# Bursts of four fills in place of three in a causal-attention loop on one Trainium2 core

## The chip, the cores and the metric

The kernel runs on one core of a Trainium2 chip. The metric is the device time of one execution in microseconds (us); the time of the kernel before is the median of 3 runs. Besides the times there is one profiled execution with a trace of every instruction. The engines are named as in the profile: PE is TensorE (matmuls) and PEld its weight loads, DVE is VectorE, ACT is ScalarE, POOL is GpSimd, and SP is the engine that issues most DMAs.

## The reference

A block of three layers on x of 8 x 1024 x 256: half a feed-forward layer, causal attention with 16 heads of 16 columns, and half a feed-forward layer again, each added to x after a layer norm. Cut to the attention and to the fact that matters about the experts:

```python
def _L0_attn_ref(x, Wq, bq, Wkv, bkv, Wo, bo):
    q = x @ Wq.T + bq                       # 16 heads of 16 columns
    k, v = jnp.split(x @ Wkv.T + bkv, 2, axis=-1)
    dots = jnp.einsum('bhid,bhjd->bhij', q * scale, k)
    attn = softmax(where(causal, MASK_VAL, dots))
    return jnp.einsum('bhij,bhjd->bhid', attn, v) ... @ Wo.T + bo

def _L0_ffn_ref(tokens, gate_w, w1, b1, w2, b2):
    ...
    keep = counts <= cap                    # an expert over its capacity is dropped whole
    valid = keep[a_e]
    ...
x = x + 0.5 * _L0_ffn_ref(_layernorm(x), ...)
x = x + _L0_attn_ref(_layernorm(x), ...)
x = x + 0.5 * _L0_ffn_ref(_layernorm(x), ...)
```

An expert that gets more tokens than its capacity contributes nothing. The kernel counts the tokens of each expert on the chip and runs the feed-forward layers only if some expert is kept; on these inputs no expert is, so the profile shows one pass of attention with the gates' arithmetic beside it.

## The kernel before

**Units.** `attention` walks 32 units: 8 batches of 4 groups of 4 heads. In each unit there are 18 fills of a kind called maxima here (M, built by `m_steps`) and 18 called exponentials (E, built by `e_steps`). The M stream runs ahead: while the E fills of unit u run, the M fills of unit u+1 do, with a lead of three fills.

**An M fill** multiplies q and k into a tile `sm` of 128 x 1024 numbers in PSUM (a few 64-row matmuls on the two halves of the array), adds the causal mask by small bf16 matmuls where a diagonal block lies in it (10 of the 18 fills; the other 8 are called plain), and then VectorE takes the row maxima (`tensor_reduce` into `mx`). **An E fill** writes minus the maxima into a tile `sc` by a matmul (`sc<-neg,take_m`), adds k by q, and ScalarE takes the exponential into `pT`.

**Three buffers.** Both kinds of tile come from one pool, `ps_pair`, of three buffers of two PSUM banks; two more banks (`ps_sum`, `ps_bank`) serve everything else, so all eight are in use. Buffers go round: a fill takes the one that the third fill before it used, and its first matmul waits until VectorE or ScalarE has read that tile.

**Bursts and gaps.** The main loop emits fills by `step`, and after every third one (`FILLS = 3`, `every`) it calls `gap`. A gap emits the other work of TensorE: up to two pieces of attention times values that are due (`pav`, from the queue `owed`; one piece if at most two are queued), and steps of projections, values and output products (`pq`, `pv`, `px`, `pta`, from the queue `work`) at a rate of 17/12 a gap (13/12 for the first batch). These matmuls use the array in four column strips (128*32 in the profile), the fills use it in two row halves (64*128). The order of a unit's fills is written out: `"EMEMEM" * 6`, that is bursts E M E and M E M by turns, 36 fills and 12 gaps. At some places `small` steps of `side` work (layer-norm statistics, gate arithmetic, most of it on VectorE) go in. If six `pT` tiles are alive, an E fill first emits the next piece of `pav` itself.

**Order.** A `Lane` wraps each engine and pins every instruction behind the one before it in the source, so each engine's order is the order in which Python emits it. The program is written as straight-line code; all of it carries the helper's line L625 in the profile.

**DMAs.** The row maxima go out and back as DMAs (`rows<-mside`, `neg<-rows`); `fetch` brings the next unit's q and k (`qk<-parts`). Their places are counted in fills (`due`, `start`).

Of the kernel before, what the change touches and what calls it, by code (L numbers as in the profile page):

```python
# [29 lines left out]
def macaron_kernel(  # L30
# [570 lines left out]
    def attention(run_no, src, dst, gate0, logits, tally):  # L601
        NU = B * NG
        VW = HD + 1
        FILLS = 3
        stack = ExitStack()
        with stack:
            ps_pair = stack.enter_context(tc.tile_pool(name=f"ps_pair{run_no}", bufs=3, space=PSUM))
# [96 lines left out]
            def biased_late(b):  # L704
                for jj in range(TB // 2):
                    biased(b, jj)
                    yield
# [35 lines left out]
            def enter(b):  # L743
                xnT = xnTs[b] = ap.tile([P, DC, S], F32, tag="xnT", name=f"xnT{b}", bufs=1)
                for jj in range(TB // 2):
                    drain(coming.pop((b, jj), ()))
                    while (b, 2 * jj + 1) not in xns:
                        take(side)
                        yield
                    pt = bank(f"pta{b}_{jj}")  # L750
                    for i in range(2):
                        xn = xns.pop((b, 2 * jj + i))
                        for c in range(DC):
                            o = (c * 2 + i) * P
                            if b:
                                product(pt[:, o : o + P], xn[:, c * P : (c + 1) * P], ident)
                            else:
                                transpose(pt[:, o : o + P], xn[:, c * P : (c + 1) * P])
                    on.scalar.copy(
                        xnT[:, :, 2 * jj * P : (2 * jj + 2) * P], pt.rearrange("p (c w) -> p c w", c=DC)  # L760
                    )
                    if b and jj + 2 < TB // 2:
                        soon(b, jj + 2)
                    yield True
# [91 lines left out]
            def gate_first(b):  # L856
                if gate0 is not None:
                    lg = gate0[0][:, b * TB : (b + 1) * TB, :]
                    both = (yield from choose(ap_route, f"f{b}", TB, lg))[2]
                    on.vector.tensor_tensor(gate0[1], gate0[1], both, ALU.add)  # L860


            def m_steps(u):
                q, k = qks[u % 3][:, 0], qks[u % 3][:, 1]
# [39 lines left out]
                plain = [(1, [(ib, 0, pr, 0)]) for pr in range(2) for ib in range(4, 8)]  # L904
# [8 lines left out]
                if u == 0:  # L913
                    todo = masked_ones[0] + plain + masked_ones[1]
                else:
                    rest = deque(masked_ones[0] + masked_ones[1])
                    plain = deque(plain)
                    todo = [(plain if n % 3 == 1 or not rest else rest).popleft() for n in range(18)]
                steps = [lambda a=a: fill(*a) for a in todo]
                done = max(n for n, a in enumerate(todo) if a[0] == 0)  # L920

# [40 lines left out]
            count = [0]  # L962
# [237 lines left out]
            def mixed(many, few):  # L1200
                n = 0
                for step in many:
                    yield step
                    n += bool(step)
                    if step and n % 2 == 0:
                        for other in few:
                            yield other
                            if other:
                                break
                yield from few  # L1210
# [5 lines left out]
            def take(works):  # L1216
                while works:
                    try:
                        return next(works[0])
                    except StopIteration:  # L1220
                        works.popleft()
                return False
# [42 lines left out]
            def gap(rate):  # L1265
                n = 0
                most = 2 if len(owed) > 2 else 1
                while owed and n < most and owed[0][0] <= count[0]:
                    owed.popleft()[1]()
                    n += 1  # L1270
                behind[0] += rate
                while behind[0] >= 1:
                    behind[0] -= 1
                    if take(work) and not spare[0]:
                        break
                behind[0] = min(behind[0], 4)

            def step(fill, every, rate, small):
                due()
                fill()  # L1280
                count[0] += 1
                small, urgent[0] = max(small, urgent[0]), 0
                for _ in range(small):
                    if take(side):
                        break
                if count[0] % every == 0:
                    gap(rate)

            def start(steps, lag=0):
                timed.append([count[0] + (3 * lag + 2) // 4, steps])  # L1290

            def due():
                for entry in list(timed):
                    while entry[0] <= count[0]:
                        lag = next(entry[1], None)
                        if lag is None:
                            timed.remove(entry)
                            break
                        entry[0] = count[0] + (3 * lag + 2) // 4

            stream = [0]
            urgent = [0]
            units = {}

            def maxima():
# [13 lines left out]

            for u in range(-1, NU):  # L1320
                b, g = divmod(u, NG)
                rate, every = (17 if b else 13) / 12, FILLS
                if u < 0:
                    pass
                elif g == 0:
                    spare[0] = False
                    if b + 1 < B:
                        work += [enter(b + 1), project(b + 1, 0)]
                        if b:
                            work.append(mixed(leave(b - 1), project(b + 1, 1)))  # L1330
                        else:
                            work.append(mixed(values_of(b + 1), project(b + 1, 1)))
                        if b:
                            work.append(values_of(b + 1))
                    if b:
                        start(divide(b - 1, 1, 0), 4)
                        after[u - 1, 1] = divide(b - 1, 1, 1)
                    side.append(gate_first(b))
                    if not b:
                        side.append(biased_late(b))  # L1340
                elif g == 1 and b + 1 == B:
                    work.append(leave(b - 1))
                elif g == 1 and b == 0:
                    side.append(biased_late(1))
                elif g == 2:
                    if b == 0:
                        start(read(2), 40)
                    if b + 1 == B:
                        start(divide(b, 0, 0), 12)
                        start(divide(b, 0, 1), 16)  # L1350
                        after[u, 0] = divide(b, 1, 0, 4, (8, 1, 6, 8))
                elif g == 3:
                    if b + 1 < B:
                        start(divide(b, 0, 0), 8)
                        start(divide(b, 0, 1), 20)
                    if b + 1 == B:
                        after[u - 1, 1] = divide(b, 1, 1, 4, (6, 1, 4, 5))
                        last_on.append(ap.tile([P, 4, P], F32, tag="wsb", name="last_on", bufs=4))
                        on.gpsimd.memset(last_on[0], 0.0)
                        rate = 8 / 3  # L1360
                if u >= 0 and u + 2 < NU:
                    start(fetch(u + 2, lag=6), 8)
                if u < 0:
                    for n in range(18):
                        step(maxima, 1, 8 / 5 if n < 5 else 16 / 13, 1)
                else:
                    if u == 0:
                        for n in range(3):
                            step(maxima, every, rate, n)
                    es = deque(e_steps(u))  # L1370
                    for k, which in enumerate("EMEMEM" * 6):
                        small = 3 if k % 6 in (1, 5) else 0
                        if which == "E":
                            step(es.popleft(), 2 if u + 1 == NU else every, rate, 0 if u + 1 < NU else 2)
                        elif stream[0] < 18 * NU:
                            step(maxima, every, rate, small)
                if g == NG - 1:
                    while work and u + 1 < NU:
                        drain(work.popleft())
# [75 lines left out]
```

## Time and profile before

| | |
|---|---|
| median of 3 runs | 1188.32 us (1184.97 to 1193.11) |
| the profiled execution | 1189.08 us, span 1187.3 us, granted PE clock 0.985 of full speed |
| busy, ACT / POOL | 734.4 us (62%) / 432.9 us (36%) |
| DVE, from 350 to 950 us | 506.3 of 600 us busy |
| PE, from 350 to 950 us | 596.5 of 600 us busy |
| PE, from 1130 us to the end | 32.2 of 57 us busy |

A busy PE is not a PE at its peak: matmuls overlap, and their ends are modelled. What a stretch costs is read from the start of one matmul to the start of the next. A row of the timeline gives the start, the time from the first start to the last end of the merged instructions, the engine, the operation, the tiles (out<-in), the shape and how many there are; what ended the idle time before it stands in brackets.

### The profile page before, as it was taken

How to read it: one execution, taken by the hardware profiler on the slowest of the kernel's cores; microseconds unless marked ns; L12 is line 12 of the kernel's file. 1: busy time of each engine (PE TensorE's matmuls, PEld its weight loads, DVE VectorE, ACT ScalarE, POOL GpSimd, SP SyncE). 2: the span in 40 equal slices, each digit the busy share in tenths (PEclk: the TensorE clock that was granted, in tenths of full speed). 3: DMA queues.
4: the chain of work that ended last, by engine and by line, in shares of the span. 5: the costliest groups of instructions: out<-in, count | busy, mean ns of one | idle time of the engine just before them, and what ended most of it. 6: DMA issues, size and time to landing. Idle time of an engine off the chain costs nothing.

```text
span 1187.3 us, 36308 instructions
## 1 busy us (share of the span) xinstructions
PE 1132.9 (95%) x15178; PEld 657.9 (55%) x15178; DVE 936.8 (79%) x1652; ACT 734.4 (62%) x955; POOL 432.9 (36%) x774
## 2 busy tenths in 40 slices
PE   7789999999999999999999999999999999999983
PEld 4355555655565555655556555555556555555541
DVE  4667778788798878888888887988788887798934
ACT  4146666666666566666666666766666666665660
POOL 6125323433344223542235333442235423232331
PEclk9889999999999999999999999999999999999997
DMA  6553455565545557355564655455473555543211
GB/s 192 199 195 124 150 177 186 171 213 162 178 143 165 189 154 219 116 179 168 180 190 135 218 163 173 144 166 197 154 226 107 183 168 176 161 133 110 74 33 39
DMA packets 108517, 190.25 MB, mean 160 GB/s; under 512 B 24752, under 2 KB 42296, under 8 KB 108344
## 3 DMA queue, kind: packets, MB, share of 16 engines
q1 hardware_dynamic: 106968, 187.24, 49.4%
q8 instruction: 122, 2.00, 0.7%
q10 hardware_dynamic: 1376, 0.59, 0.2%
q14 instruction: 51, 0.42, 0.1%
HBM read 94.50 MB, written 93.31 MB: 158 GB/s over the span
## 4 chain that ended last, share of the span: by engine, by line
PE 80%; DMA 7%; DVE 7%; POOL 2%; ACT 1%; issue 1%; SPq 1%; ACTq 0%; POOLq 0%; DVEq 0%
PE sc L625 24%; PE pav L625 23%; PE sm L625 15%; PE pq L625 8%; PE pv L625 4%; PE px L625 4%; DVE mx L625 4%; PE pta L625 2%; DMA parts<-high 2%; DMA neg<-rows 1%; DMA parts<-split 1%; DMA rows<-mside 1%; DMA qk<-parts 1%; SPq L625 1%; POOL x_a L625 1%
## 5 line engine op out<-in xcount | busy, mean ns | idle before, releaser
L625 DVE TENSOR_REDUCE mx<-sm 128x2 f32<-128x1024 f32 (+2 forms) x576 | 686.5, 1217 | 167.6 <-PE sm L625 166.6
L625 ACT ACTIVATE pT<-sc 128x1024 f32<-128x1024 f32 x576 | 572.5, 1022 | 301.1 <-PE sc L625 292.2
L625 PE MATMUL pav<-pT,vaug 128*32 128x256 f32 (+3 forms) x4608 | 327.9, 387 | 2.2 <-ACT att L625 1.4
L625 POOL TENSOR_SCALAR_AFFINE_SELECT pT<-pT 128x256 f32<-128x256 f32 (+1 forms) x448 | 190.6, 441 | 308.5 <-ACT pT L625 307.2
L625 PE MATMUL sc<-neg,take_m 64*128 64x512 f32 x1152 | 265.7, 456 | 15.2 <-DVE mx L625 5.8
L625 PE MATMUL sm<-qk 64*128 64x512 f32 (+3 forms) x1536 | 264.7, 381 | 7.3 <-DMA qk<-parts 7.2
L625 PE MATMUL sc<-qk 64*128 64x512 f32 (+3 forms) x1536 | 229.6, 334 | 0.0
L625 PEld LDWEIGHTS sm<-qk 64*128 64x128 f32 x1536 | 139.5, 187 | 107.8 <-issue 47.5
L625 POOL TENSOR_TENSOR low<-whole,high 128x512 f32<-128x512 f32 x60 | 77.0, 1283 | 285.0 <-ACT high L625 278.8
L625 PEld LDWEIGHTS pav<-pT,vaug 128*32 128x32 f32 x4608 | 113.9, 109 | 104.6 <-issue 52.7
L625 PEld LDWEIGHTS sc<-neg,take_m 64*128 64x128 f32 x1152 | 109.9, 185 | 110.0 <-issue 56.2
L625 PEld LDWEIGHTS sc<-qk 64*128 64x128 f32 x1536 | 146.9, 186 | 15.6
L625 PE MATMUL sm<-masked,before_k 64*128 64x128 bf16 (+1 forms) x1280 | 86.9, 213 | 0.0
L625 PE MATMUL px<-woT,on 128*32 128x264 f32 x1024 | 74.8, 387 | 0.9 <-ACT on L625 0.9
L625 PE MATMUL pv<-wvT,xnT 128*32 128x264 f32 x1024 | 75.4, 391 | 0.0
L625 PE MATMUL pq<-xnT,wkT 128*32 128x256 f32 x1024 | 75.0, 389 | 0.0
L625 PE MATMUL pq<-xnT,wqT 128*32 128x256 f32 x1024 | 74.4, 389 | 0.5 <-ACT xnT L625 0.5
L625 PEld LDWEIGHTS <-before_k 64*128 64x128 bf16 x1280 | 38.5, 96 | 45.6 <-issue 29.9
L625 POOL TENSOR_TENSOR x_a<-x_a,bo_all 128x512 f32<-128x512 f32 x32 | 41.5, 1303 | 23.6 <-DVE xn_a L625 23.6
L625 PEld LDWEIGHTS pq<-xnT,wqT 128*32 128x32 f32 x1024 | 33.2, 112 | 29.2 <-issue 11.3
L625 PEld LDWEIGHTS px<-woT,on 128*32 128x32 f32 x1024 | 34.4, 110 | 26.8 <-issue 10.8
L625 PEld LDWEIGHTS pv<-wvT,xnT 128*32 128x32 f32 x1024 | 32.2, 110 | 26.3 <-issue 7.3
(133 smaller groups left out, 732.1 us busy)
## 6 DMA issues: line engine op xcount, KB each, us to landing
qk<-parts SPq DMA_DIRECT2D x124, 512.0 KB
parts<-high SPq DMA_DIRECT2D x120, 256.0 KB
parts<-low SPq DMA_DIRECT2D x120, 256.0 KB
sums<-att SPq DMA_DIRECT2D x62, 256.0 KB
out_dram<-x_a SPq DMA_DIRECT2D x16, 512.0 KB
x_a<-in_L_attn_x_dram SPq DMA_DIRECT2D x15, 512.0 KB
on<-sums SPq DMA_DIRECT2D x30, 256.0 KB
rs<-inv SPq DMA_DIRECT2D x30, 256.0 KB
```

Of the source, the lines that this page charges most:

```text
L625: i = call(*args, **kwargs)
```

## The change

The unit's order becomes `"MEEM" * 9`: M, two E, M, and then a gap. `FILLS` becomes 4, so that a unit has 9 gaps, and the rate of other work becomes 17/9 a gap (13/9 in the first batch). The two `small` places of three side steps in six fills become one of four in four, at the end of a burst. The count of fills at which a gap falls now starts where unit 0 begins (`first`). Within a unit's 18 M fills, plain and masked ones now alternate, and not one plain one among three.

```diff
-        FILLS = 3
+        FILLS = 4
...
-                    todo = [(plain if n % 3 == 1 or not rest else rest).popleft() for n in range(18)]
+                    todo = [(plain if (n % 2 == 1 and plain) or not rest else rest).popleft() for n in range(18)]
...
-                if count[0] % every == 0:
+                if (count[0] - first[0]) % every == 0:
                     gap(rate)
...
             urgent = [0]
+            first = [0]
...
-                rate, every = (17 if b else 13) / 12, FILLS
+                rate, every = (17 if b else 13) / 9, FILLS
...
                     if u == 0:
                         for n in range(3):
-                            step(maxima, every, rate, n)
+                            step(maxima, 1 if n == 2 else 99, rate, n)
+                        first[0] = count[0]
                     es = deque(e_steps(u))
-                    for k, which in enumerate("EMEMEM" * 6):
-                        small = 3 if k % 6 in (1, 5) else 0
+                    for k, which in enumerate("MEEM" * 9):
+                        small = 4 if k % 4 == 3 else 0
```

## The prediction

> **What bounds the kernel now.** I read the page's busy shares and its chain of waits first.
>
> ```profile
> PE 1132.9 (95%) x15178; PEld 657.9 (55%) x15178; DVE 936.8 (79%) x1652; ACT 734.4 (62%) x955; POOL 432.9 (36%) x774
> PE 80%; DMA 7%; DVE 7%; POOL 2%; ACT 1%; issue 1%; SPq 1%; ACTq 0%; POOLq 0%; DVEq 0%
> ```
>
> TensorE is busy nearly all the time and carries 80% of the chain that ended last; between 350 and 950 us it is busy 596.5 of 600. Whatever makes TensorE wait inside this loop lengthens the kernel, and whatever it no longer does shortens it.
>
> Second, the timeline of one burst M E M: what a change of array form costs, and when the first tile is read.
>
> ```profile
> 509.31 0.51 PE L625 MATMUL sm<-qk 64*128 64x512 f32 x2
> 509.64 0.39 PE L625 MATMUL sc<-neg,take_m 64*128 64x512 f32 x2
> 509.85 2.36 DVE L625 TENSOR_REDUCE mx<-sm 128x2 f32<-128x1024 f32 x2 [0.94 <-PE sm L625]
> 509.87 0.40 PE L625 MATMUL sc<-qk 64*128 64x512 f32 x2
> 510.10 0.40 PE L625 MATMUL sm<-qk 64*128 64x256 f32 x4
> 510.34 0.29 PE L625 MATMUL sm<-masked,before_k 64*128 64x128 bf16 x4
> 510.56 0.64 PE L625 MATMUL pav<-pT,vaug 128*32 128x256 f32 x8
> ```
>
> From start to start a pair of 512 columns takes 0.23 us (509.87 to 510.10), but the first of the burst 0.33. The three fills are through at 1.25. VectorE reads the first tile from 0.54 after the burst began, and two reductions take 2.36: the first ends at about 1.74. The burst is over by then, so TensorE doesn't care.
>
> Third, the one place after the start-up where six fills M E M E M E ran without a gap:
>
> ```profile
> 1067.26 0.50 PE L625 MATMUL sm<-qk 64*128 64x512 f32 x2
> 1067.62 0.50 PE L625 MATMUL sc<-neg,take_m 64*128 64x512 f32 x2
> 1067.96 0.40 PE L625 MATMUL sc<-qk 64*128 64x256 f32 x4
> ...
> 1068.34 2.34 DVE L625 TENSOR_REDUCE mx<-sm 128x2 f32<-128x1024 f32 x2
> ...
> 1069.61 0.50 PE L625 MATMUL sc<-neg,take_m 64*128 64x512 f32 x2 [0.84 <-DVE mx L625]
> 1069.94 0.39 PE L625 MATMUL sc<-qk 64*128 64x512 f32 x2
> ```
>
> The fourth fill needs the first fill's buffer. The first reduction ended near 1069.51 (half of 2.34 after 1068.34), the fourth fill began at 1069.61, and TensorE stood still for 0.84 us.
>
> **The change part by part.** All burst figures below are start-to-start times collected over every burst of the trace before. It has 398 bursts, which take 565 us from their first fill to the next other matmul: 153 of form E M E with a masked M (mean 1.617 us, 247 us), 153 M E M with a masked M at the end (1.353, 207), 31 + 31 without a mask (1.438 and 1.129, 80), and 30 others (31). The median pieces of M E M, masked, are 0.339 (first M), 0.468 (E) and 0.462 (masked M up to the next work).
>
> The changed kernel's instruction order, built but not run, has 338 bursts in the pass that executes: 217 M E E M with a plain first M and a masked last one, 30 with both masked, 30 M E E that break off because six `pT` tiles are alive (a piece of `pav` comes out, then M alone), 40 M alone (those 30, and 10 in the first unit's lead-in), and 21 odd ones. The number of matmuls is the same. So 60 bursts go, not the 96 that three gaps in each of 32 units would make.
>
> *What it removes.* Leaving a burst costs 0.09 (0.32 from the last `sc` to other work, 0.23 to another fill), entering costs 0.11 in the gap (0.31 in place of 0.20 between products) and 0.10 in the first fill: 0.30 a burst. Sixty times that is 18 us. A masked M in the middle costs the next E some 0.08 (E M E exits: 0.641 with a mask, 0.559 without); 153 such become 30: 123 x 0.08 = 10 us. The rest of what the sum below gains is that I put medians for the new bursts, without some 20 us that the means before hold over their medians (waits for `neg<-rows` and buffers; slower bursts give those DMAs more time).
>
> The Trainium skill, "TensorEngine Tiling (Array Packing)", Key Properties, says that a change of tiling mode drains the array, and "TensorE: Matmul & The Clock Gate", Single matmul latency, puts a drain near 175 ns. By that estimate two changes a burst would give 60 x 0.35 = 21 us where the rows give 18.
>
> *What it adds.* The wait. The changed order's semaphores say that each fill waits for the reader of the third fill before it: of a burst's last M that is the reduction of its own first M. Unstalled, that last M would start at 0.339 + 0.468 + 0.468 = 1.275. In the 184 bursts that begin with M now, the reduction starts 0.538 (tenth percentile), 0.543 (median), 0.63 (mean) after the burst and takes 1.22; it ends at 1.765, 1.770 and 1.85. A held fill restarts 0.05 to 0.10 after the reduction's end. So the last M starts at about 1.92 and TensorE waits 0.65, in each burst. It cannot be below 1.765 + 0.05, however idle VectorE is. Behind the held M stand, on TensorE's queue, the whole gap: `pav`, projections, output products, and ScalarE's evictions of those. Nothing can pass.
>
> A burst M E E M then takes 1.85 + 0.07 + 0.49 (0.46, and half of the 0.10 that a restart may pay) = 2.41. With a masked first M I add up 0.49 + 0.57 + 0.47 unstalled; its reduction ends near 1.91, and the burst takes 2.48. M E E: 0.339 + 0.468 + 0.55 = 1.36. M alone 0.82.
>
> Sum: 217 x 2.41 = 523, 30 x 2.48 = 74, 30 x 1.36 = 41, 40 x 0.82 = 33, others 19: 690 us against 565, +125. Sixty entries of 0.11 lie outside the bursts: -7. Together +118.
>
> The Trainium skill, "Perfetto Trace Analysis", Optimization Strategy, speaks against this change: the same bubble repeating on the saturated engine can mean that PSUM has no room for the next tile. It has no price for it.
>
> *What I cost at nothing.* The bunched side steps: VectorE's work a burst is 936.8/288 = 3.25 us; a burst and its gap will last some 4.4, so VectorE should be free when the next first M is done. If it isn't, each 0.1 us of lateness costs 247 x 0.1 = 25 us. ScalarE has two exponentials in a row (2 x 1.02, ending about 3.1 after the burst began); their buffers are wanted in the next burst, after 4.4. The gap's work is the same amount in nine pieces. SP's DMAs are placed by fills, and fills come slower.
>
> Bounds: with the reduction never late (1.765, restart 0.05, last M 0.46) M E E M takes 2.28; 30 x 2.40; the sum is 660, +88 in all. With VectorE 0.15 later than its mean now: 118 + 247 x 0.15 = +155.
>
> The profiled execution took 1189.08, 0.1% over the median; the forecast is 1189 + 118 = 1307.
>
> **The rivals.** *Faster: the last M doesn't wait.* If two E fills covered the reduction, the bursts would take 217 x 1.735 + 30 x 1.99 + 41 + 33 + 19 = 529 us, -36 and -7: 1146. That is decided at 1.275 us after the burst begins: the reduction would have to be over by then. None of the 184 was over before 1.76, and the reduction alone takes 1.15 at least. It remains only if the buffers don't go round as the order says. 5%.
>
> *VectorE falls behind.* The four side steps, done at once behind the last M's reduction, delay the next first M's reduction by as much as one reduction (1.22) in half of the bursts: 124 x 1.22 = +151 more, about 1458. For it: VectorE is 84% busy between 350 and 950 us. Against: the longer period makes its share lower, some 74%. 7%.
>
> *The wait is partly made good.* TensorE's idle time before and the waits in gaps shrink further than I put it, or VectorE begins on first tiles 0.28 earlier, as it does on masked fills within a burst (0.26 after the last matmul's start, and 0.54 after a plain one's): 247 x 0.28 = 69 off, 1238. Against: ScalarE too begins 0.49 after the last 512-column matmul of an E, so it's the length of the matmul that sets this. 6%.
>
> **How the numbers follow.** The forecast gets 82%. Its own bounds are 1189 + 88 = 1277 and 1189 + 155 = 1344; a little more room below, for waits made good, gives 1268 to 1345, and about 2 in 10 stay outside. The point is taken at 1305. Measurements of this kernel spread by 0.7% in all, so 1% is what can be told from no change. Faster by over 1%: the first rival, 5%. Slower: the forecast and the other two, less a little for waits made good altogether: 93%. Within 1%: 2%.
>
> **What would show it.** In the waits, fills (`sm`) held by VectorE's `mx` should be the largest cause of TensorE's idle time, some 250 times, some 0.5 us of idle matmul time each (0.65 less the modelled overlap). TensorE's busy time should stay near 1130 us while its share falls below 90%. From a burst's first M to its last M there should be about 1.9 us, and the restart should follow the first reduction's end within 0.1. The granted clock should stay where it is. I'm wrong if the last M starts near 1.3; too low if reductions of first Ms start well after 0.63; too high if the gaps before held waits that vanish.

## The result and the profile after

The changed kernel takes 1382.33 us (median of 4 runs, 1379.78 to 1385.26) where the kernel before takes 1187.66 in the same runs: a ratio of 1.162, with a 95% interval of 1.159 to 1.166. The forecast was 1305 in 1268 to 1345: the direction was right, the size was not. The profiled execution took 1379.78 us, with a span of 1378.0.

The page of the changed kernel, its busy shares and its chain by engine:

```profile
PE 1165.9 (85%) x15178; PEld 673.2 (49%) x15178; DVE 948.9 (69%) x1652; ACT 726.3 (53%) x955; POOL 433.0 (31%) x774
PE 41%; DVE 41%; DMA 5%; POOL 5%; ACT 4%; issue 3%; SPq 1%; ACTq 0%; POOLq 0%; DVEq 0%
```

No engine has more instructions than before, and every engine's share is lower. What held 80% of the chain, TensorE, now shares it evenly with VectorE: the two hand the work to each other. What TensorE waits for (engine, tile, what it waited for: us in total, times, longest):

```profile
PE sm L625 <- DVE mx L625: 128.6, 229, 2.8
PE pav L625 <- POOL pT L625: 23.1, 28, 0.9
PE sm L625 <- ACT pT L625: 16.0, 17, 5.4
...
PE pta L625 <- DVE xn_a L625: 6.4, 8, 0.9
```

Before, the fills waited 5.8 us in nine places for VectorE's maxima. Now 229 M fills do. One burst of the changed kernel, from its timeline, the matmuls of TensorE and the work of VectorE:

```profile
603.40 0.50 PE L625 MATMUL sm<-qk 64*128 64x512 f32 x2
603.74 0.40 PE L625 MATMUL sc<-neg,take_m 64*128 64x512 f32 x2
603.89 0.23 DVE L625 TENSOR_TENSOR tally<-tally,both_g 128x64 f32<-128x64 f32 x1
603.97 0.39 PE L625 MATMUL sc<-qk 64*128 64x512 f32 x2
604.03 0.21 DVE L625 TENSOR_REDUCE mx_f<-logits 128x8 f32<-128x64 f32 x1
604.20 0.39 PE L625 MATMUL sc<-neg,take_m 64*128 64x512 f32 x2
604.28 0.23 DVE L625 TENSOR_TENSOR lc_f<-logits,mx_f 128x64 f32<-128x64 f32 x1
604.42 1.22 DVE L625 TENSOR_REDUCE mx<-sm 128x2 f32<-128x1024 f32 x1
604.43 0.39 PE L625 MATMUL sc<-qk 64*128 64x512 f32 x2
605.70 0.50 PE L625 MATMUL sm<-qk 64*128 64x512 f32 x2 [0.88 <-DVE mx L625]
606.04 0.23 PE L625 MATMUL sm<-masked,before_k 64*128 64x64 bf16 x4
```

The fourth fill would follow at 604.66. Its buffer is the first fill's, and the reduction of that ended at 605.64; the fill starts 0.06 later. This burst shows a second thing: the reduction could have begun at 603.94 (0.54 after the burst), but VectorE was still doing side steps, which the program puts behind the last M of the burst before. It began at 604.42.

Of the 216 bursts M E E M with full records, 198 restart like this one, 0.05 to 0.06 us after their own first reduction, and three start later. In the other 15 the fourth fill starts before the first one has been read. One of them:

```profile
475.06 0.50 PE L625 MATMUL sm<-qk 64*128 64x512 f32 x2
...
476.07 1.94 ACT L625 ACTIVATE pT<-sc 128x1024 f32<-128x1024 f32 x2 [1.80 <-PE sc L625]
...
477.15 0.55 PE L625 MATMUL sm<-qk 64*128 64x128 f32 x4 [0.60 <-ACT pT L625]
...
477.31 2.35 DVE L625 TENSOR_REDUCE mx<-sm 128x2 f32<-128x1024 f32 x2
```

The first M is read only from 477.31. The last M starts at 477.15, 0.06 after the first of the two exponentials has ended (one takes 1.02), so it has that E's buffer. Buffers do not go strictly round in these 15, whose first reductions start 0.9 to 1.7 us late. In the kernel before no fill starts ahead of the reader of the third fill before it.

Where the 194 us went (from the first burst to the last, start to start, collected over the trace as in the prediction):

| | forecast | measured |
|---|---|---|
| 217 bursts M E E M, masked at the end | 523 (2.41 each) | 568 (216 with full records: least 2.32, median 2.44, mean 2.63) |
| 30 with both M masked | 74 | 74 |
| 30 M E E, broken off | 41 | 42 |
| 40 M alone | 33 | 24 |
| others (measured: with the 217th M E E M, 4 us) | 19 | 25 |
| all bursts, against 565 before | +125 | +168 |
| gaps | -7 | +25 (560 before, 585 after) |
| together | +118 | +194 |

### The profile page after: what moved, and what is told of

The parts are those of the page before. It is cut to its first block, busy times and chain, and to the rows that moved or that the text cites. A ratio compares the mean times of both kernels' runs of the same rounds, so it can differ in the third digit from the quotient of the medians.

```text
span 1378.0 us, 36234 instructions
## 1 busy us (share of the span) xinstructions
PE 1165.9 (85%) x15178; PEld 673.2 (49%) x15178; DVE 948.9 (69%) x1652; ACT 726.3 (53%) x955; POOL 433.0 (31%) x774
## 4 chain that ended last, share of the span: by engine, by line
PE 41%; DVE 41%; DMA 5%; POOL 5%; ACT 4%; issue 3%; SPq 1%; ACTq 0%; POOLq 0%; DVEq 0%
DVE mx L625 29%; PE sm L625 14%; PE pav L625 13%; PE pq L625 6%; POOL pT L625 2%; PE pv L625 2%; DVE mneg L625 2%; ACT pT L625 2%; PE px L625 2%; PE pta L625 1%; DMA parts<-high 1%; PE sc L625 1%; POOL low L625 1%; DVE st_g L625 1%; DVE xn_a L625 1%
## 5 line engine op out<-in xcount | busy, mean ns | idle before, releaser
L625 DVE TENSOR_REDUCE mx<-sm 128x2 f32<-128x1024 f32 (+2 forms) x576 | 701.1, 1220 | 340.0 <-PE sm L625 338.5
L625 ACT ACTIVATE pT<-sc 128x1024 f32<-128x1024 f32 x576 | 558.3, 1021 | 353.9 <-PE sc L625 347.7
L625 PE MATMUL sm<-qk 64*128 64x512 f32 (+3 forms) x1536 | 297.8, 425 | 149.9 <-DVE mx L625 128.6
L625 PEld LDWEIGHTS sm<-qk 64*128 64x128 f32 x1536 | 130.3, 185 | 371.1 <-DVE mx L625 226.0
L625 PE MATMUL sc<-neg,take_m 64*128 64x512 f32 x1152 | 235.8, 405 | 3.7 <-DMA neg<-rows 1.6
L625 ACT COPY vaug<-pv 128x256 f32<-128x256 f32 x64 | 23.9, 374 | 98.2 <-PE pv L625 98.2
L625 PE MATMUL px<-woT,on 128*32 128x264 f32 x1024 | 68.9, 386 | 0.2 <-ACT on L625 0.2
L625 PE MATMUL pq<-xnT,wkT 128*32 128x256 f32 x1024 | 67.5, 380 | 0.0
L625 ACT ACTIVATE whole<-pq,bqT 128x512 f32<-128x512 f32 x32 | 22.0, 688 | 60.5 <-PE pq L625 57.8
L625 DVE TENSOR_TENSOR x_a<-px,x_a 128x256 f32<-128x256 f32 x64 | 26.1, 407 | 31.1 <-PE px L625 30.5
```

Source lines behind the costliest of these rows:

```text
L625: i = call(*args, **kwargs)
```

## The experiments

Each run is compared with runs of the kernel before on the same chip. The last column of this table is the median time; intervals are those of the ratio.

| run | what it is | us | ratio, 95% |
|---|---|---|---|
| | before | 1187.5 to 1188.8 | |
| | the change | 1382.3 | 1.159 to 1.166 |
| e1 | change, plain maxima over half the keys | 1285.9 | 1.079 to 1.086 |
| e2 | change, masked maxima over half the keys | 1329.1 | 1.116 to 1.122 |
| e3 | change, order E M E M | 1376.4 | 1.156 to 1.164 |
| e4 | before, kinds in pairs, bursts of three | 1261.8 | 1.059 to 1.066 |
| e5 | change, side steps two and two | 1361.8 | 1.143 to 1.152 |
| e6 | change, gaps stop at an end piece | 1339.6 | 1.124 to 1.131 |
| e11 | e5 and e6 together | 1303.8 | 1.095 to 1.101 |
| e7 | e11, all maxima over half the keys | 1187.6 | 0.998 to 1.001 |
| e8 | before, all maxima over half the keys | 1179.8 | 0.990 to 0.995 |
| e9 | e11, all maxima over a quarter | 1161.6 | 0.975 to 0.981 |
| e10 | before, all maxima over a quarter | 1182.1 | 0.994 to 0.997 |

Softmax does not depend on which number is subtracted before the exponential, so a maximum over part of the keys changes the length of VectorE's reduction and little else. It protects less against overflow; inputs on which that matters were not tried.

**Is it the first reduction, or VectorE's load? (e1, e2)** A mirrored pair: both shorten about half of VectorE's reductions, but only one of them those that the last M waits for.

```diff
# e1 (e2 has "if ends:")
+                    if not ends:
+                        in_ = in_[:, :, ::2] if len(pieces) == 1 else in_[:, :, :, ::2]
                     on.vector.tensor_reduce(out, in_, AX.X, ALU.max)
```

> The changed kernel, but the row maxima of the 8 plain fills of a unit are taken over every second column only (the maximum is then that of half the keys; the masked fills keep all). Theory (a burst's last M waits for its own first M's reduction): the first reduction takes about 0.65 us in place of 1.22 and ends 1.2 after the burst began, before the last M is wanted at 1.28, so nearly all of the wait goes: 216 bursts from 2.63 to some 1.8 us, -180, about 1200 (1185 to 1230). Rival V (VectorE's load as a whole): VectorE has 256 x 0.57 = 146 us less work, and it falls here too, but it must then fall at least as much when the masked fills are halved. Rival O (the order M E E M and the 9 gaps cost the time, not the buffer): no more than 20 us off, 1360 or more.

> The changed kernel, but the row maxima of the 10 masked fills of a unit are taken over every second column only (the plain fills keep all). These are the last M of most bursts and the first M of 30. Theory: first reductions are as long as before; only their lateness (some 45 us in all) shrinks, and 30 bursts with a masked first M gain 0.5 each: 1325 to 1375. Rival V: VectorE has 320 x 0.57 = 182 us less work, more than with the plain fills halved, so at least as much comes off: 1200 or less. Rival O: 1360 or more.

e1 took 96 us off, e2 53, though e2 relieves VectorE of more (789.8 us busy against 823.0). So load alone is not it, and rival O, who allowed 20 us, is out. e2 fell where the theory put it: the 30 bursts with a masked first M went from 2.475 to 1.929 us (-16 in all), the others from 2.630 to 2.494, as their first reductions became more punctual (64 us late in all before, 20 in e2). But e1 missed its range by 56 us. Its timeline, VectorE, shows the reduction as short as supposed:

```profile
603.11 0.69 DVE L625 TENSOR_REDUCE mx<-sm 128x2 f32<-128x512 f32 x1 [1.93 <-PE sm L625]
604.48 1.23 DVE L625 TENSOR_REDUCE mx<-sm 128x2 f32<-128x1024 f32 x1 [0.67 <-PE sm L625]
```

That burst began at 602.57, the last M at 603.86 and the next work at 604.37: 1.80 us. The median of M E E M was 1.90, yet the mean 2.17: 216 x 0.27 = 58 us of bursts whose first reduction began late. And the gaps were as long as in the change (589 us). In e1 the first reductions were late by 67 us in all, as much as the change's 64, though VectorE had 126 us less to do. It is what stands ahead of a reduction that makes it late, and e2 shortens just that, the last M's reduction. The theory had one wait, and there were three.

**Is it the order of the kinds? (e3, e4)**

```diff
# e3, from the change
-                    for k, which in enumerate("MEEM" * 9):
+                    for k, which in enumerate("EMEM" * 9):
# e4, from the kernel before, with the change's alternation of plain and masked
-                    for k, which in enumerate("EMEMEM" * 6):
+                    for k, which in enumerate("EMMEEM" * 6):
```

> The changed kernel with the order E M E M in each burst of four (9 gaps, rates and side steps as in the change). Theory: the fourth fill now waits for the exponential of the first E, which starts 0.83 and ends 1.86 after the burst began; wanted at 1.27, so again some 0.6 us a burst, and less jitter since ScalarE does less beside: 1340 to 1390. Rival O: the order of before is back, so the time comes back to 1185 to 1230. Rival V: VectorE is no longer in the chain within a burst, 1200 to 1260.

> The kernel before with bursts of three and 12 gaps, but with fills of a kind in pairs (E M M and E E M by turns) and plain and masked M alternating as in the change. Theory: no fill needs a buffer that was filled in its own burst, so no wait of this kind: 1185 to 1225. Rival O (pairs of one kind, alternation of masks): most of the loss is here too, 1300 or more.

e3 came out at 1376.4, as the theory said: with an E first, the last M waits for ScalarE in the same places. Its waits of TensorE:

```profile
PE sm L625 <- ACT pT L625: 134.4, 254, 1.1
PE pav L625 <- ACT att L625: 23.9, 30, 1.2
```

e4 fell between the two expectations, 74 us above the kernel before. Bursts of three have no wait within the burst, but the last M of E E M needs the buffer that the last M of the burst before filled, and VectorE was late with that. Its timeline, VectorE first, then TensorE:

```profile
599.70 1.23 DVE L625 TENSOR_REDUCE mx<-sm 128x2 f32<-128x1024 f32 x1
600.84 0.42 DVE L625 BATCH_NORM_STATS2 st_g<-x_a 128x6 f32<-128x256 f32 x1
601.29 0.18 DVE L625 BATCH_NORM_AGGREGATE mv_g<-st_g 128x2 f32<-128x6 f32 x1
601.39 0.39 DVE L625 BATCH_NORM_STATS2 st_g<-x_a 128x6 f32<-128x256 f32 x1
601.82 0.18 DVE L625 BATCH_NORM_AGGREGATE mv_g<-st_g 128x2 f32<-128x6 f32 x1
601.91 1.19 DVE L625 TENSOR_REDUCE mx<-sm 128x2 f32<-128x1024 f32 x1
```

```profile
602.33 0.40 PE L625 MATMUL sc<-qk 64*128 64x512 f32 x2
603.16 0.50 PE L625 MATMUL sm<-qk 64*128 64x512 f32 x2 [0.44 <-DVE mx L625]
```

Layer-norm statistics, side steps, stand between the two reductions, and the second is 1 us later than it need be. Over the 185 bursts E E M it begins 0.5 us late in the mean, and side steps are nearly all that runs in between. A reduction that is put behind side steps costs TensorE time even where three buffers would do.

**VectorE's lateness and the gaps (e5, e6, e11).** In the change, the first reduction of a burst starts late behind four side steps in a row. Beside the burst above, one of the six cases with the longest steps, four layer-norm applications, from the timeline (some of its rows):

```profile
388.43 1.18 DVE L625 TENSOR_REDUCE mx<-sm 128x2 f32<-128x1024 f32 x1
389.39 0.50 PE L625 MATMUL sm<-qk 64*128 64x512 f32 x2
389.53 2.33 DVE L625 TENSOR_SCALAR xn_a<-x_a,mv_a,rstd_a 128x256 f32<-128x256 f32 x4
390.34 1.36 POOL L625 TENSOR_TENSOR x_a<-x_a,bo_all 128x512 f32<-128x512 f32 x1 [0.83 <-DVE xn_a L625]
391.78 1.21 DVE L625 TENSOR_REDUCE mx<-sm 128x2 f32<-128x1024 f32 x1
```

The reduction was due at 389.93 and began at 391.78. In all, 88 of the 216 first reductions start more than 0.1 us late. Of the 64 us between the time due and the start, VectorE spent 44 on side steps, 9 on the adds to x and the logits that gaps put there, 6 on other reductions and the settling of the maxima; 5 it was idle. TensorE lost only 44 of the 64, because 20 fall to the 15 bursts whose last M had another buffer.

The gaps' +25 us have another place, from the timeline between two units:

```profile
610.71 0.64 PE L625 MATMUL pav<-pT,vaug 128*32 128x256 f32 x8
...
611.42 0.58 ACT L625 COPY att<-pav 128x512 f32<-128x512 f32 x1
...
612.15 1.06 PE L625 MATMUL pav<-pT,vaug 128*32 128x512 f32 x8 [0.80 <-POOL pT L625]
```

The last `pav` piece of one unit and the first of the next come out in the same gap. The accumulator `ps_sum` has one bank, so the second waits until ScalarE has copied it out. The row names GpSimd's selects, which end at nearly the same time, but it is the copy that sets the start: in all 30 such places of this trace, and in the 30 of e3's, `pav` starts 0.145 us after the copy's end, while the selects end anywhere from 0.004 to over 0.2 us before it. In the kernel before a burst lies between them. That is another resource with too few buffers for what is put in a row, and it is 28 x 0.8 us. A smaller wait of the gaps grew too: `pta` waited 6.4 us for VectorE's `xn_a`, 0.6 before.

```diff
# e5
-                        small = 4 if k % 4 == 3 else 0
+                        small = 2 if k % 4 in (0, 3) else 0
# e6: an entry of owed also carries `end`
                 while owed and n < most and owed[0][0] <= count[0]:
-                    owed.popleft()[1]()
                     n += 1
+                    last_piece = owed[0][2]
+                    owed.popleft()[1]()
+                    if last_piece:
+                        break
```

> The changed kernel with the four side steps of a burst in two places: two after the first M, two after the last (small = 2 at k % 4 of 0 and 3). In the changed kernel's trace the 216 bursts M E E M last 2.319 us at least and 2.630 in the mean; the difference, 67 us in all, is put down to first reductions that start late, behind four side steps queued on VectorE after the last M's reduction. If so, two steps at a time let most of them start in time: 30 to 45 us off, 1335 to 1352. Rival (they are late because of what the gaps put on VectorE, the adds to x and the logits, or for no reason of place): 1372 to 1390.

> The changed kernel, but a gap stops after a piece of attention times values that ends a half (so that the next half's first piece comes one burst later and the copy out of the single accumulator bank lies under that burst). Theory of the gaps' +25 us: 28 times that first piece stood behind the end piece in one gap and waited 0.8 us, 23 us in all, for ScalarE's copy and GpSimd's selects. These go; and by the order 30 more bursts now break off with a piece of attention times values between E and the last M, which hides the wait there: 0.4 net each, -12. Together 1335 to 1355. Rival (the gaps got longer by pieces and products in another way, or the wait only moves): 1370 to 1390.

> The changed kernel with full maxima, side steps two and two and gaps that stop at an end piece: the two repairs together, alone 20.5 and 42.8 us. Theory: they mend different waits and add up, 1382 - 63 = 1319 (1308 to 1330); what is left over the kernel before, some 130 us, is the wait that the three buffers set. Rival (both mend the same waits): 1335 or more.

e5 took 20.5 us off: the sign is the theory's, the size isn't. M E E M went from 2.63 to 2.57 only. The lateness of first reductions did fall from 64 to 37 us, and its part by side steps from 44 to 13. But what TensorE waited for of it fell only from 44 to 35: the 15 bursts that had another buffer have become 2. What is left is the settling of the maxima (12 us; four steps in a row that the kernel urges), side steps and the gaps' adds. The bursts gave 11 of the 20 us and the gaps 7. e6 took 42.8 off, in its range and by its two parts: the gaps fell from 585 to 564 us and the bursts from 734 to 712, more than the 12 expected of them. Together they gave 78.5, more than the 63 of the sum and outside the range; the bursts fell by 41 and the gaps by 38, where the two runs alone make 33 and 29. The two help each other, and I have no run that says how. What is left, 116 us over the kernel before, is mostly the wait that three buffers set: M E E M still takes 2.43 in the median.

**What a burst of four is worth without its waits (e7 to e10).** These leave out half or three quarters of the keys in all maxima.

```diff
# e7 and e8 with ::2, e9 and e10 with ::4
+                    in_ = in_[:, :, ::2] if len(pieces) == 1 else in_[:, :, :, ::2]
                     on.vector.tensor_reduce(out, in_, AX.X, ALU.max)
```

> The changed kernel with all row maxima over every second column (half of the keys), side steps two and two, and gaps that stop at an end piece. Theory: the three waits of the change (the first reduction, VectorE behind, the accumulator bank) are gone; the bursts take 187 x 1.82, 30 x 2.0, 60 x 1.41, 70 x 0.61 and some 25 us, 553 in all against 565 before, and the gaps lose their 25: 1160 to 1190, and no gain over the kernel before with the same maxima by more than 1%. Rival (bursts of four are better by 42 us once nothing waits, as the first rival of the prediction has it): 1146 or less.

> The kernel before with all row maxima over every second column (half of the keys): the control for what the shorter maxima alone do. VectorE isn't in the way there: only the some 20 us that burst means hold over their medians can go, 1165 to 1188. If VectorE's load bound the kernel before (rival V), it would fall by 100 or more.

> As the kernel with all three (maxima over part of the columns, side steps two and two, gaps that stop at an end piece), but the maxima over every fourth column (a quarter of the keys). With every second column the first reduction still ended at 1.23 us, and the last M, wanted at 1.28 with its weights loaded ahead, started at 1.30 and took 0.57 to the next work, where 30 last Ms that weren't held took 0.47. Theory: with a reduction of about 0.4 us the first ends at 0.95, no last M is held, M E E M takes 1.74 as the prediction's first rival had it, 186 x 0.16 = 30 us less than with half the columns: 1150 to 1165. Rival (the four-fill burst has another cost of its own that isn't the reduction): 1178 or more.

> The kernel before with the maxima over every fourth column: the control for the run with a quarter of the keys in bursts of four. Theory: with half the columns 1179.8, and nothing in a burst of three waits for a reduction, so no more than 3 us come off: 1175 to 1181. Rival V: a further 50 us or more.

Three of the four came out as the theory had them; e10, at 1182.1, is 1 us above its range, and far from the 50 us less of rival V. The kernel before gains 0.4% to 0.8% from shorter maxima, so VectorE's reductions were not what bounded it. The bursts of four go from 1303.8 (full maxima) to 1187.6 (half) to 1161.6 (a quarter): with half the keys they are still 0.7% behind their control e8, and with the first reduction out of the way they beat the kernel before, by 2.2%, and their control e10, by 1.7%. A burst of e9, TensorE:

```profile
503.18 0.50 PE L625 MATMUL sm<-qk 64*128 64x512 f32 x2
503.51 0.40 PE L625 MATMUL sc<-neg,take_m 64*128 64x512 f32 x2
503.75 0.39 PE L625 MATMUL sc<-qk 64*128 64x512 f32 x2
503.98 0.39 PE L625 MATMUL sc<-neg,take_m 64*128 64x512 f32 x2
504.20 0.39 PE L625 MATMUL sc<-qk 64*128 64x512 f32 x2
504.43 0.45 PE L625 MATMUL sm<-qk 64*128 64x128 f32 x4
504.72 0.29 PE L625 MATMUL sm<-masked,before_k 64*128 64x128 bf16 x4
```

The last M starts 1.25 after the first and nothing is bracketed; such bursts take 1.76 us in the median.

## Why the prediction was right and wrong

*The mechanism* was right. The last M waits for the reader of the third fill before it, in 228 of the 246 bursts of both kinds that have full records; the first reduction ended 1.77 us after the burst in the median, as read from the trace before; the held M restarted 0.055 after it. The least M E E M is 2.32 where the bound said 2.28. e1 against e2, e3, and e9 show that it is this wait.

*What the burst removes* was right in sign and too large: e9 against e10 gives 20 us where the first rival's sum had 43. By the traces, e9's bursts take 7 us less than e10's and its gaps 12, where that sum had 36 and 7. e9 has 30 more broken bursts than that sum, so the two are not quite the same thing.

*The step that failed* is "What I cost at nothing". It held that VectorE "should be free when the next first M is done", by an average: 3.25 us of work in a period of 4.4. The average was right, and says nothing on order. The four side steps stand in one place, ahead of the one reduction that TensorE waits for: the last M started 2.07 after the burst in the mean where I had 1.92, 216 x 0.15 = 32 us. Of these, 6.6 are a single burst at the start, at 63 us, whose last M waited for an exponential. I had used the lateness of the kernel before, 0.09, although the change moves those very steps; the gaps' adds to x, which I did not name, stand there too. The same paragraph took the gap's work as "the same amount in nine pieces": it is, but in nine gaps two pieces that share the accumulator's bank meet, and the gaps gained 25 us where I had -7. The upper bound, +155, allowed for 0.15 us of lateness and so for the first of these two; it held nothing for the gaps' 32 us, and those and the next term are what lies beyond it.

*A smaller term:* after its wait the last M took 0.56 to the next work where I put 0.49, 216 x 0.07 = 15 us. In e2, 30 last Ms that didn't wait took 0.47, against 0.50 in the change. A held fill's weights are held too: the weight loads of M fills waited for VectorE's maxima 267 times, 226 us in all. The M alone were cheaper than put, 24 us and not 33. The rows 32, 32 and 15, less 9, with 6 for the odd bursts, are the 76 us between +118 and +194.

*The rivals.* The second, VectorE behind by a whole reduction in half of the bursts, was too strong: the least and the median burst are punctual, and 88 of the 216 bursts start their reduction late, by 0.7 us in the mean. But it named the place that I then priced at nothing. The third, part of the wait made good, didn't come.

## What to carry to other kernels

Count buffers along a burst: with n buffers going round, the fill n+1 waits for the reader of the first, and the price is when that reader ends after the burst began, less when the fill is wanted, times the bursts; read it off the bursts that already exist. Then ask what stands in the reader's queue just ahead of it in the new order: an average load under 100% does not make an engine punctual. And where work is bunched into fewer gaps, look which pieces of it now touch that share a single buffer.

## What the runs showed of the hardware

The reduction's time goes by the elements it reads, also where they lie apart: 1.22 us for 1024 a partition, 0.69 for every second, 0.42 for every fourth.

VectorE's instructions can be several times longer beside GpSimd's long ones. `xn_a` takes 0.41 us, but up to 1.37 in the change, six times of 64; the median and the largest before are 0.41 and 0.56. In e11, all 30 VectorE instructions that took over 0.3 us more than their kind's median, 26 us in all, ended within 0.2 us of the end of a GpSimd `tensor_tensor` of 1.3 to 1.7 us; in the change, 14 of 16. The fourth step of the case at 389.53 above is one: it took 1.36, up to 391.86, beside the GpSimd row that ended at 391.70. "SBUF — State Buffer", SBUF: two separate sides, in the Trainium skill, says why this can be: the two engines share a pair of ports, and the one whose instruction takes it first holds it for the whole instruction while the other is blocked. The traces agree in the times; no run took GpSimd's work away, so that it is this lock was not shown.
